# Reordered start of a four-layer graph-attention kernel: first nodes and layer 0's weights ahead, the other layers' preparation behind the first projections

## The chip, the cores and the metric

One core of one Trainium2 chip runs the whole kernel. The metric is device microseconds (us) of one execution. Of the kernel before, three first runs gave a median of 3268.11 us (3267.7 to 3269.8). Runs are sorted into a fast and a slow state by their time. Each comparison of times is made within one call, on one chip; a comparison of two profiles can be across calls and chips, and two profiles of one kernel differ by about 1 us at the start (see b0_before and c0_after).

## The reference, cut to what matters

```python
# x (16, 1024, 256) f32, adj (16, 1024, 1024) int32 in {0, 1}
def layernorm(x): m, v = mean(x), var(x); return (x - m) / sqrt(v + 1e-5)

# layers 0, 1, 2 (they differ in the edge function and in an elu at the end)
h   = maximum(layernorm(x), 0)
Wh  = h @ W                                  # (1024, 256) @ (256, 256) for each of 16 batches
e   = leaky_relu((Wh @ a1)[:, :, None] + (Wh @ a2)[:, None, :], 0.2)
att = softmax(where(adj == 0, NEG, e), axis=-1)
x   = x + einsum('bij,bjo->bio', att, Wh)
# layer 3: four heads of 64, a_src and a_dst of shape (4, 5, 64) of which only type 0 is met,
# then relu, bias, a layernorm with gamma and beta over each head, and x + that
```

## The kernel before

The kernel handles 16 batches as two interleaved streams. A batch needs its nodes `x_b` (1 MB), its adjacency as eight tiles of 128 rows (loaded with a cast to bf16, squared for a check on ACT, transposed on PE, cast into `mask` on ACT), then for each layer a projection (`project`), edge weights (`weigh`, on DVE) and the sums over neighbours (`attend`, on PE). The instruction order on each engine is not the order of the source: a scheduler settles it when the kernel is built.

```python
    ident_b = const.tile([P, P], BF, name="ident_b")
    nc.vector.tensor_copy(ident_b, ident)               # needed by every adjacency transpose
    ...
    def load(b: int):
        xs[b] = nodes.tile([P, NI, D], F32, name="x_b")
        nc.sync.dma_start(xs[b], x[b].rearrange("(i p) f -> p i f", p=P))
        masks[b] = nodes.tile([P, NI, N], U8, name="mask")
        def fetch(i: int):
            fetched[i] = adjs.tile([P, N], BF, name="adj_i")       # three buffers
            nc.gpsimd.dma_start(fetched[i], adj[b, ts(i, P), :])
        for i in range(AHEAD):                                     # AHEAD = 2
            fetch(i)
        yield
        for i in range(NI):                                        # NI = 8
            if i + AHEAD < NI:
                fetch(i + AHEAD)
            adj_i = fetched.pop(i)
            nc.scalar.activation(every, adj_i, AF.Square, ..., accum_out=squares[:, b, i : i + 1])
            turned = psum.tile([P, NI, P], BF, name="misc", bufs=3)
            for j in range(NI):
                nc.tensor.transpose(turned[:, j, :], adj_i[:, ts(j, P)], ident_b)
            nc.scalar.copy(masks[b][:, :, ts(i, P)], turned)
            yield

    # loads of W0..W3, bias, gamma, beta on SP: all ahead of the first nodes
    for l in range(3): nc.sync.dma_start(W[l][:, :, :D], ...)
    ...
    for _ in load(0):                                              # x_b of batch 0 and its masks
        pass
    nc.vector.tensor_scalar_add(beta, beta, -2.0)
    with tc.tile_pool(name="prep", bufs=2) as prep:                # all layers: W x a on DVE
        for l in range(3): ...  # load a_b; tensor_tensor_reduce(prod, W, a_b, accum_out=wa)
        for s, name in enumerate(("L3_a_src", "L3_a_dst")): ...    # load 640 KB, use a fifth of it
        ...                     # columns of W from wa, and a check of the norms on PE
    ...
    def batch(b: int):
        ...
        for n in range(NI // 2 + 2):                               # project layer 0, four pairs of tiles
            for pair in range(max(n - 2, 0), min(n + 1, NI // 2)):
                yield from islice(pairs[pair], 1)
        ...
        V = yield from attend(0, V, finish0, 1)
```

In `attend` each edge weight tile `w[:, j, :]` (128x512, made on DVE) feeds four sums of 128 rows:

```python
            for j in range(NI):
                nc.tensor.matmul(acc, w[:, j, ts(i % NG, P)], V[:, j, : D + 1],   # 128x257, f32
                                 start=(j == 0), stop=(j == NI - 1))
```

## Time and profile before

The timeline gives the marks that the argument runs on. All are us from the start of the span.

| mark | before |
|---|---|
| first statistics of the nodes (nodes landed) | 17.77 |
| adjacency tile 0 turned | 16.3 |
| tile 3 fetched / tile 7 fetched | 16.9 / 27.3 |
| first projection of layer 0 | 38.62 |
| first edge weight | 46.89 |
| product records 1, 17 and 41 of the first sums | 48.46, 53.14, 58.36 |
| end | 3266.97 |

A "record" is one matmul entry of the trace, in the group of the sums `acc<-V,weights`. The program has 3072 such products (3 layers, 16 batches, 64 each) and the profile lists 6144, so a product of 128x257 in f32 is two records. One weight tile thus feeds eight records in the end. This line of the timeline of the kernel before (columns: start, us, engine, line, operation, output and inputs, shapes, count) is a reading that the prediction passed over:

```profile
50.47 9.79 PE L346 MATMUL acc<-V,weights 128*128 128x257 f32 x44
```

From 50.47 us on PE takes 44 records without a gap, 0.22 us each. The weights are not all there yet at that time, but PE is full.

### The profile page before, as it was taken

The page shows a single profiled execution, that of the slowest core. Times are in us where ns is not written, and L with a number is a line of the kernel's source. Part 1 is how long each engine was busy: PE and PEld are TensorE (multiplying, and loading weights), DVE is VectorE, ACT ScalarE, POOL GpSimd, SP SyncE. Part 2 cuts the span into 40 slices and gives each one's busy share as a digit, 9 for nine tenths or more (in the row PEclk, how much of TensorE's full clock was granted, in tenths as well). Part 3 has the DMA queues.
Part 4 walks back from the last instruction along what each step waited for, and adds up shares of the span by engine and source line. Part 5 has one row for each costly group of instructions (what it writes and reads, how often), then busy time and mean ns, then how long its engine had stood idle before and what let it go on. Part 6 is the DMA issues. An engine that isn't in the chain of part 4 may idle for free.

```text
span 3267.0 us, 38466 instructions
## 1 busy us (share of the span) xinstructions
PE 3075.9 (94%) x13702; PEld 2129.5 (65%) x13702; DVE 2546.5 (78%) x6140; ACT 969.5 (30%) x2081; POOL 1086.2 (33%) x1286
## 2 busy tenths in 40 slices
PE   6999999999999999999999999999999999999987
PEld 5776766657666676666766667676676766767562
DVE  5778787777877778877788877888778787787767
ACT  3423323232332323323233232322323223232121
POOL 1323424233242332423334233342323423233242
PEclk8999999999999999999999999999999999999998
DMA  4101101011010111100111010110101101000000
GB/s 118 27 4 17 33 12 41 7 16 30 14 39 7 17 29 17 36 10 13 30 17 36 10 17 28 15 36 13 39 4 17 33 13 40 4 14 13 1 13 14
DMA packets 55190, 73.18 MB, mean 22 GB/s; under 512 B 4048, under 2 KB 37968, under 8 KB 54992
## 3 DMA queue, kind: packets, MB, share of 16 engines
q0 software_dynamic: 18432, 33.56, 7.0%
q1 hardware_dynamic: 36560, 37.10, 3.6%
q8 instruction: 110, 1.80, 0.2%
q14 instruction: 88, 0.72, 0.1%
HBM read 87.43 MB, written 16.78 MB: 32 GB/s over the span
## 4 chain that ended last, share of the span: by engine, by line
PE 70%; DVE 18%; POOL 6%; issue 2%; ACT 2%; DMA 1%; SPq 0%; ACTq 0%; POOLq 0%
PE acc L346 31%; PE acc L427 22%; PE projected L242 11%; DVE weights L262 8%; PE misc L235 2%; PE misc L254 2%; POOL x_b L282 2%; DVE centered L227 2%; DVE stats L222 2%; POOL rstd L213 1%; PE misc L122 1%; DVE above L280 1%; DVE above L281 1%; DMA adj_i<-in_adj_dram 1%; POOL y L407 1%
## 5 line engine op out<-in xcount | busy, mean ns | idle before, releaser
L346 PE MATMUL acc<-V,weights 128*128 128x257 f32 x6144 | 1440.8, 384 | 8.4 <-DVE weights L262 7.0
L346 PEld LDWEIGHTS acc<-V,weights 128*128 128x128 f32 x6144 | 1139.5, 191 | 205.0 <-DVE weights L262 38.6
L427 PE MATMUL acc<-weights,V 128*65 128x512 f32 x2048 | 913.2, 594 | 0.3 <-DVE weights L262 0.3
L262 DVE SCALAR_TENSOR_TENSOR weights<-row,ex,mask 128x512 f32<-128x512 f32 x1024 | 744.9, 776 | 36.7 <-ACT row L258 36.7
L262 DVE SCALAR_TENSOR_TENSOR weights<-row,V,mask 128x512 f32<-128x512 f32 x768 | 593.4, 815 | 49.3 <-ACT row L258 47.9
L213 POOL TENSOR_TENSOR rstd<-rstd,minus_half 128x2 f32<-128x2 f32 (+1 forms) x320 | 330.2, 1034 | 883.3 <-DVE rstd L212 834.9
L427 PEld LDWEIGHTS acc<-weights,V 128*65 128x65 f32 x2048 | 279.4, 138 | 499.4 <-issue 477.2
L242 PE MATMUL projected<-W,hT 128*128 128x259 f32 (+1 forms) x2048 | 522.3, 397 | 40.8 <-DVE V L297 24.9
L242 PEld LDWEIGHTS projected<-W,hT 128*128 128x128 f32 x2048 | 388.1, 195 | 137.0 <-DVE V L297 37.5
L282 POOL TENSOR_TENSOR x_b<-x_b,above 128x256 f32<-128x256 f32 x256 | 222.1, 868 | 478.9 <-DVE above L281 436.6
L278 ACT ACTIVATE below<-acc,inv 128x256 f32<-128x256 f32 x256 | 121.0, 473 | 657.1 <-DVE inv L271 463.5
L222 DVE BATCH_NORM_STATS2 stats<-x_b 128x6 f32<-128x256 f32 x512 | 209.3, 415 | 126.0 <-POOL x_b L282 121.1
L235 PE MATMUL misc<-ident,centered 128*128 128x128 f32 x1024 | 168.5, 281 | 75.7 <-DVE centered L227 70.3
L237 ACT COPY hT<-misc 128x512 f32<-128x512 f32 x256 | 147.2, 588 | 299.6 <-PE misc L235 298.9
L227 DVE TENSOR_SCALAR centered<-x_b,mv 128x256 f32<-128x256 f32 x512 | 229.6, 451 | 4.7
L431 ACT COPY sums<-acc 65x512 f32<-65x512 f32 x128 | 74.1, 579 | 513.9 <-PE acc L427 512.4
L235 PEld LDWEIGHTS misc<-ident,centered 128*128 128x128 f32 x1024 | 120.8, 143 | 128.2 <-DVE centered L227 107.9
L258 ACT COPY row<-misc 128x512 f32<-128x512 f32 x224 | 129.8, 587 | 196.2 <-PE misc L254 196.0
L106 POOL DMA_DIRECT2D adj_i<-in_adj_dram x128 | 77.6, 606 | 287.4 <-ACT sums L431 214.6
L280 DVE TENSOR_SCALAR above<-acc,inv 128x256 f32<-128x256 f32 x256 | 122.8, 480 | 61.8 <-ACT below L278 60.9
L392 POOL TENSOR_TENSOR y<-y,bias 128x512 f32<-128x512 f32 x64 | 90.5, 1414 | 234.2 <-DVE y L439 215.9
L293 ACT ACTIVATE V<-projected,rstd 128x3 f32<-128x3 f32 x384 | 99.3, 263 | 228.0 <-PE projected L242 227.4
(70 smaller groups left out, 2311.4 us busy)
## 6 DMA issues: line engine op xcount, KB each, us to landing
adj_i<-in_adj_dram POOLq DMA_DIRECT2D x128, 256.0 KB, 3.9
x_b<-in_x_dram SPq DMA_DIRECT2D x16, 1024.0 KB, 7.9
out_dram<-y SPq DMA_DIRECT2D x32, 512.0 KB, 3.6
W<-in_L_gnn_W_dram SPq DMA_DIRECT2D x3, 256.0 KB, 3.6
a_b<-in_L_gnn_a_dram SPq DMA_DIRECT2D x3, 256.0 KB, 7.4
a_b<-in_L_gnn_a_src_dram SPq DMA_DIRECT2D x1, 640.0 KB, 8.4
a_b<-in_L_gnn_a_dst_dram SPq DMA_DIRECT2D x1, 640.0 KB, 10.2
W<-in_L_gnn_W_dram SPq DMA_DIRECT2D x2, 128.0 KB, 9.4
```

The lines of the kernel that those rows point to most:

```text
L213: nc.gpsimd.tensor_tensor(r, r, minus_half.to_broadcast([P, n]), op=ALU.pow)
L222: nc.vector.bn_stats(stats, xb[:, 2 * pair + n, :])
L227: nc.vector.tensor_scalar(centered[:, n, :], xb[:, 2 * pair + n, :], mv[:, n, 0:1], 0.0, op0=ALU.subtract, op1=ALU.max,)
L235: nc.tensor.transpose(turned[:, k, ts(n, P)], centered[:, n, ts(k, P)], ident)
L237: nc.scalar.copy(hT, turned)
L242: nc.tensor.matmul(projected, hT[:, k, ts(n, P)], W[l][:, k, :], start=(k == 0), stop=(k == NK - 1),)
L258: nc.scalar.copy(r, turned)
L262: nc.vector.scalar_tensor_tensor(w[:, j, :], r, c(j), mask[:, j, ts(half, HALF)], op0=op, op1=ALU.mult)
L280: nc.vector.tensor_scalar(above, acc[:, :D], inv, 0.0, op0=ALU.mult, op1=ALU.max)
L282: nc.gpsimd.tensor_add(xi, xi, above)
L346: nc.tensor.matmul(acc, w[:, j, ts(i % NG, P)], V[:, j, : D + 1], start=(j == 0), stop=(j == NI - 1),)
L427: nc.tensor.matmul(accT, V3[:, j, h, :], w[:, j, :], start=(j == 0), stop=(j == NI - 1))
```

## The change

Its intent is to start the real work of the first batch earlier: the nodes of batch 0 and layer 0's W and a go to the head of the load queue, in the source the other layers' loads and DVE preparation come behind the first projections, and so does batch 0's mask work. Layer 3's two vectors are loaded without the four fifths that nobody reads, and temporary tiles come from pools that exist anyway. The diff, cut to its core:

```diff
@@ the loads and the preparation become a generator
-    for l in range(3):
-        nc.sync.dma_start(W[l][:, :, :D], ins[f"L{l}_W"].rearrange("(k p) o -> p k o", p=P))
-    ... (W3, bias, gamma, beta)
-    for _ in load(0):
-        pass
-    nc.vector.tensor_scalar_add(beta, beta, -2.0)
-    with tc.tile_pool(name="prep", bufs=2) as prep:
-        ... (products of W and a of all layers)
-            nc.sync.dma_start(
-                a_b3.rearrange("p h t e -> p (h t e)"), on_all_partitions(ins[name], H * T * E)
-            )
+    def prepare():
+        scratch = edges.tile([P, NI, HALF], F32, name="weights")
+        def fetch(l: int): ...                       # W and a of layer l
+                    bass.AP(tensor=first.tensor, offset=first.offset, ap=[[0, P], [T * E, H], [1, E]]),
+        fetch(0)
+        for l in range(3):
+            if l == 0:
+                yield
+            fetch(l + 1)
+            ... (products of W and a of layer l)
+            extend(l)
+            yield
+        ... (layer 3, and only then beta, and the check of the norms)
@@ def batch(b)
+        if b == 0:
+            next(preparing)                          # layer 0's preparation only
@@ after the projections of layer 0
+        if b == 0:
+            for _ in chain(loading, preparing):      # masks of batch 0, then layers 1 to 3
+                pass
@@ before the streams start
+    loading, preparing = load(0), prepare()
+    next(loading)                                    # x_b of batch 0, tiles 0 and 1
+    next(preparing)                                  # W0, a0
```

More of the change, by code (lines that the diff above doesn't have):

```diff
@@ L23 @@
 from contextlib import ExitStack
-from itertools import islice
+from itertools import chain, islice
 import concourse.bass as bass
@@ L99, in load @@
         nc.sync.dma_start(xs[b], x[b].rearrange("(i p) f -> p i f", p=P))
-        masks[b] = nodes.tile([P, NI, N], U8, name="mask")
+        mask = masks[b] = nodes.tile([P, NI, N], U8, name="mask")
         fetched = {}
@@ L122, in load @@
                 nc.tensor.transpose(turned[:, j, :], adj_i[:, ts(j, P)], ident_b)
-            nc.scalar.copy(masks[b][:, :, ts(i, P)], turned)
+            nc.scalar.copy(mask[:, :, ts(i, P)], turned)
             yield
-    W = [const.tile([P, NK, D + e], F32, name=f"W{l}") for l, e in enumerate(EXT)]
-    for l in range(3):
-        nc.sync.dma_start(W[l][:, :, :D], ins[f"L{l}_W"].rearrange("(k p) o -> p k o", p=P))
-    for k in range(NK):
-        nc.sync.dma_start(
-            W[3][:, k, :D].rearrange("p (h e) -> p h e", h=H),
-            ins["L3_W"][:, ts(k, P), :].rearrange("h p e -> p h e"),
-        )
+    edges = ctx.enter_context(tc.tile_pool(name="edges", bufs=4))
+    rows = ctx.enter_context(tc.tile_pool(name="rows", bufs=4))
+    single = ctx.enter_context(tc.tile_pool(name="single", bufs=1))
+    work = ctx.enter_context(tc.tile_pool(name="work", bufs=3))
+    small = ctx.enter_context(tc.tile_pool(name="small", bufs=6))
+    W = [const.tile([P, NK, D + e], F32, name=f"W{l}") for l, e in enumerate(EXT)]
+    wa = const.tile([P, NK, 3 + H, 2], F32, name="wa")
     bias = const.tile([P, D], F32, name="bias")
@@ L137, in short_path @@
     beta = const.tile([P, D], F32, name="beta")
-    for t, a in ((bias, ins["L3_bias"]), (gamma, ins["L3_gamma"]), (beta, ins["L3_beta"])):
-        nc.sync.dma_start(t, on_all_partitions(a, D))
-    for _ in load(0):
-        pass
-    nc.vector.tensor_scalar_add(beta, beta, -2.0)
-    wa = const.tile([P, NK, 3 + H, 2], F32, name="wa")
-    with tc.tile_pool(name="prep", bufs=2) as prep:
-        for l in range(3):
-            a_b = prep.tile([P, 2, D], F32, name="a_b")
-            nc.sync.dma_start(
-                a_b.rearrange("p s o -> p (s o)"), on_all_partitions(ins[f"L{l}_a"], 2 * D)
-            )
-            for k in range(NK):
-                for s in range(2):
-                    prod = prep.tile([P, D], F32, name="prod")
-                    nc.vector.tensor_tensor_reduce(
-                        prod, W[l][:, k, :D], a_b[:, s, :], op0=ALU.mult, op1=ALU.add,
-                        scale=1.0, scalar=0.0, accum_out=wa[:, k, l, s : s + 1],
-                    )
-        for s, name in enumerate(("L3_a_src", "L3_a_dst")):
-            a_b3 = prep.tile([P, H, T, E], F32, name="a_b3")
-            nc.sync.dma_start(
-                a_b3.rearrange("p h t e -> p (h t e)"), on_all_partitions(ins[name], H * T * E)
-            )
-            for k in range(NK):
-                prod3 = prep.tile([P, H, E], F32, name="prod3")
-                nc.vector.tensor_mul(
-                    prod3, W[3][:, k, :D].rearrange("p (h e) -> p h e", h=H), a_b3[:, :, 0, :]
-                )
-                nc.vector.tensor_reduce(wa[:, k, 3:, s], prod3, AX.X, ALU.add)
+    def prepare():
         forms = [
@@ L177, in short_path, with extend @@
         ]
-        for l, form in enumerate(forms):
+        scratch = edges.tile([P, NI, HALF], F32, name="weights")
+        def extend(l: int):
             n = EXT[l] // 3
-            for c, factor in enumerate(form):
+            for c, factor in enumerate(forms[l]):
                 nc.vector.tensor_scalar_mul(
@@ L185, in short_path, with fetch @@
                 )
-        wa2 = prep.tile([P, NK, 3 + H, 2], F32, name="wa2")
-        nc.vector.tensor_mul(wa2, wa, wa)
+        def fetch(l: int):
+            if l < 3:
+                nc.sync.dma_start(
+                    W[l][:, :, :D], ins[f"L{l}_W"].rearrange("(k p) o -> p k o", p=P)
+                )
+                nc.sync.dma_start(scratch[:, l, :], on_all_partitions(ins[f"L{l}_a"], 2 * D))
+                return
+            for k in range(NK):
+                nc.sync.dma_start(
+                    W[3][:, k, :D].rearrange("p (h e) -> p h e", h=H),
+                    ins["L3_W"][:, ts(k, P), :].rearrange("h p e -> p h e"),
+                )
+            for s, name in enumerate(("L3_a_src", "L3_a_dst")):
+                first = ins[name]
+                nc.sync.dma_start(
+                    scratch[:, 3, ts(s, D)].rearrange("p (h e) -> p h e", h=H),
+                    bass.AP(tensor=first.tensor, offset=first.offset, ap=[[0, P], [T * E, H], [1, E]]),
+                )
+            for t, a in ((bias, ins["L3_bias"]), (gamma, ins["L3_gamma"]), (beta, ins["L3_beta"])):
+                nc.sync.dma_start(t, on_all_partitions(a, D))
@@ new lines, in prepare @@
+        fetch(0)
[3 more added lines that the diff above has]
+            fetch(l + 1)
+            for k in range(NK):
+                for s in range(2):
+                    prod = work.tile([P, D], F32, name="above", bufs=2)
+                    nc.vector.tensor_tensor_reduce(
+                        prod, W[l][:, k, :D], scratch[:, l, ts(s, D)], op0=ALU.mult, op1=ALU.add,
+                        scale=1.0, scalar=0.0, accum_out=wa[:, k, l, s : s + 1],
+                    )
+            extend(l)
+            yield
@@ new lines, in prepare @@
+        for s in range(2):
+            for k in range(NK):
+                prod = work.tile([P, D], F32, name="above", bufs=2)
+                nc.vector.tensor_mul(prod, W[3][:, k, :D], scratch[:, 3, ts(s, D)])
+                nc.vector.tensor_reduce(
+                    wa[:, k, 3:, s], prod.rearrange("p (h e) -> p h e", h=H), AX.X, ALU.add
+                )
+        extend(3)
+        nc.vector.tensor_scalar_add(beta, beta, -2.0)
+        groups = (3 + H) * 2
+        wa2 = small.tile([P, NK, groups], F32, name="wa2", bufs=1)
@@ L189, in short_path @@
+        nc.vector.tensor_mul(wa2, wa.rearrange("p k g s -> p k (g s)"), wa.rearrange("p k g s -> p k (g s)"))
         norms = psum.tile([P, 3 + H, 2], F32, name="misc", bufs=3)
@@ L191, in short_path @@
             nc.tensor.matmul(
-                norms.rearrange("p g s -> p (g s)"), ones,
-                wa2[:, k].rearrange("p g s -> p (g s)"), start=(k == 0), stop=(k == NK - 1),
+                norms.rearrange("p g s -> p (g s)"), ones, wa2[:, k],
+                start=(k == 0), stop=(k == NK - 1),
             )
-        both = prep.tile([P, 3 + H], F32, name="both")
+        both = small.tile([P, 3 + H], F32, name="both", bufs=1)
         nc.vector.tensor_reduce(both, norms, AX.X, ALU.add)
-        worst = prep.tile([P, 1], F32, name="worst")
+        worst = small.tile([P, 1], F32, name="worst", bufs=1)
         nc.vector.tensor_reduce(worst, both, AX.X, ALU.max)
         nc.vector.tensor_scalar(bad, worst, REACH * REACH / (2.0 * D), None, op0=ALU.is_gt)
-    edges = ctx.enter_context(tc.tile_pool(name="edges", bufs=4))
-    rows = ctx.enter_context(tc.tile_pool(name="rows", bufs=4))
-    single = ctx.enter_context(tc.tile_pool(name="single", bufs=1))
-    work = ctx.enter_context(tc.tile_pool(name="work", bufs=3))
-    small = ctx.enter_context(tc.tile_pool(name="small", bufs=6))
+        yield
     def inverse_root(var: bass.AP, n: int, eps: float, scale: float = 1.0) -> bass.AP:
```

## The prediction

> **What bounds the kernel now.** I read the page's engine totals first, then busy time by stretch, then the waits and the timeline of the first 60 us, because the change touches nothing later.
>
> ```profile
> PE 3075.9 (94%) x13702; PEld 2129.5 (65%) x13702; DVE 2546.5 (78%) x6140; ACT 969.5 (30%) x2081; POOL 1086.2 (33%) x1286
> ```
>
> PE is busy 94% of 3267 us, so 191 us are idle in the whole program. The stretches (columns: us, then busy us of PE, PEld, DVE, ACT, POOL, granted clock, DMA share, GB/s) say where:
>
> ```profile
> 0.00:16.00 16.00, 0.67 (x7) 0.77 (x8) 0.68 (x5) 2.52 (x3) 2.52 (x9) 1.00 0.88 220
> 16.00:24.00 8.00, 2.47 (x25) 2.21 (x23) 6.23 (x34) 5.48 (x8) 1.62 (x3) 0.84 0.94 277
> 24.00:36.00 12.00, 5.52 (x42) 4.35 (x40) 5.71 (x33) 10.16 (x15) 3.82 (x6) 0.50 1.06 271
> 36.00:50.50 14.50, 14.00 (x61) 11.34 (x62) 8.13 (x22) 8.05 (x20) 1.99 (x3) 0.80 0.26 43
> ```
>
> Before 36 us PE works 0.67 + 2.47 + 5.52 = 8.7 us: 27 us of idleness, all that a better start can win from. In the same 36 us the 16 DMA engines are about 0.9 busy or more, ACT is nearly full from 24 on, and DVE is busy 12.6 us. The waits of PE before 50.5 us:
>
> ```profile
> PE misc L122 <- DVE ident_b L84: 15.3, 1, 15.3
> PE misc L122 <- DMA adj_i<-in_adj_dram: 10.5, 4, 5.5
> ```
>
> The timeline shows the chain behind them:
>
> ```profile
> 14.85 0.29 DVE L143 TENSOR_SCALAR beta<-beta 128x256 f32<-128x256 f32 x1 [13.65 <-DMA beta<-in_L_gnn_ln_beta_dram]
> 15.06 0.22 DVE L84 CAST ident_b<-ident 128x128 bf16<-128x128 f32 x1
> 15.33 2.72 PE L122 MATMUL misc<-ident_b,adj_i 128*128 128x128 bf16 x24 [15.33 <-DVE ident_b L84]
> ...
> 16.88 0.54 POOL L106 DMA_DIRECT2D adj_i<-in_adj_dram  x1 [13.25 <-PE misc L122]
> ...
> 33.88 1.03 PE L122 MATMUL misc<-ident_b,adj_i 128*128 128x128 bf16 x8 [1.02 <-DMA adj_i<-in_adj_dram]
> ...
> 36.04 2.79 PE L235 MATMUL misc<-ident,centered 128*128 128x128 f32 x12 [0.36 <-DVE mv L223]
> ...
> 46.89 1.41 DVE L262 SCALAR_TENSOR_TENSOR weights<-row,V,mask 128x512 f32<-128x512 f32 x2
> ```
>
> DVE waits 13.65 us for beta, needed only in layer 3; the cast ident_b stands behind it, the transposes of adjacency tile 0 behind that, and the fetch of tile 3 (three buffers) behind those. Tile 7 is turned at 33.88; only then does the first projection start, and the edge weights of layer 0 start at 46.89. The eighth weight tile is ready at about 53.9 (four by 50.8, four more from 51.14), the first sum of eight products ends then, and PE is nearly full from there on. So **53.9 us is the mark to move**.
>
> **What the Trainium skill says.** (1) "DMA: Bandwidth & Descriptors", Queues, rings and completion order: each DMA engine takes turns between its queues, packet by packet. The trace agrees: from 4 to 10 us the software queue (adjacency) has about 0.7 of the engine time and the SP queue 0.3, though SP has plenty queued. (2) Same page, Specifications: under 512 B a DMA does not reach line rate. The trace's packets agree mildly: 256 B take 19 ns, 1 KB 52 ns, so 13 against 20 B/ns. (3) "TensorE: Matmul & The Clock Gate", Part 1: an idle PE runs at half clock and needs a busy window of 3.4 us to get the full one. The trace agrees: clock 0.50 in 24 to 36 us, 1.00 from 41.9 us, with short stretches of half clock, 3.4 or 6.8 us each, later.
>
> **The change part by part.** The order of instructions of both kernels, taken from the builds, differs only at the start: the first 204 rows of PE, 122 of DVE, 35 of ACT, 23 of POOL; after that each engine's list is the same. So whatever is won is a rigid shift of the rest.
>
> *Transfers.* Packet times of the trace: 1 KB 52 ns, 2 KB 90, 5 KB 200, 256 B 19, an adjacency packet 172. Layer 3's two vectors shrink from 256 packets of 5 KB (256 x 200 / 16 engines = 3.2 us) to 1024 of 256 B (1.2 us): 2.0 us saved. The rest is the same data in another order. Nodes go first: 1024 packets, 500 of them before the first adjacency data (seen at 3.8 us here), the others in turn with 384 adjacency packets at 224 ns a pair over 16 engines, 5.4 us, so nodes land at about 9.7 us instead of 17.77. Layer 0's W (0.8) and a (0.7) follow: 11.3 us. Each later layer takes 1.5 us; W3 1.2, a3 1.2, bias, gamma, beta 1.2: done at about 18, with the next two batches' nodes until 25.
>
> *DVE from 9.7 us*, in the new order: two tiles' statistics and centering to 11.8; layer 0's four products at 0.35 and three small writes to 13.7; ident_b; three pairs' statistics at 1.35 to 18.3; layer 1's preparation and then two evictions (L297, 0.54 each) to 21.1; then layers 2 and 3 with the other six evictions mixed in: 1.9 + 3.2 (eight of 0.37 to 0.42) + 3.2 and small writes, to about 30.
>
> *PE and the mask.* Here the gain is given back in part. In PE's new list tile 0's transposes stand behind pair 1's projections, which wait for the eviction of pair 0 (two projected buffers) at 21.1. So tile 0 is turned by 22.6 rather than 16.9, and tile 3 is fetched 6 us *later* than before. Tile 1's last two transposes stand behind pair 3's projections: 27.6. Tiles 4, 5 and 6 are then fetched at 27.7, 28.8 and 29.8 and land about 4 us later (3.9 median on the page, since the DMA engines are then free; it was 6.6 under load).
>
> *ACT* is then the last limit. It is in order: it waits for tile 3 and then has the last small evictions, until 29. From there three mask casts at 1.0 (to 32.0), then tiles 4 to 7 at 1.15 + 0.19 for the square and 1.0 for the cast, 2.15 a tile by their starts in the timeline: 8.6 us, to 40.7 (tile 7, fetched once tile 4's square is done at 33.4, has landed by 37.5, so it fits). The row copy (0.6) after it: 41.3 to 42.
>
> *Result.* First weight from 42.0 at the latest, eight at 0.67 now with no evictions between: 47.4. Mark moved by 53.9 - 47.4 = 6.5 us. Against it, PE was hardly busy from 30 to 42 us and starts the sums at half clock; while the weights pace it (0.67 against some 0.43 for a product at half clock) nothing is lost, afterwards up to one window's rest; I take 0.7 us. **Sum: 6 us won, 3268.1 - 6 = 3262 us, 0.2%.** The lists' sums of work hardly change (2.0 us of DMA work, off the path from there on).
>
> **Rivals.** (a) *The adjacency chain is not delayed*, because evictions come earlier than I have them: then tile 7 lands near 32 and weights start near 36, as if the last ACT part began 5 us sooner; the win is 11 to 12 us, 3257. For it: DMA work before tile 7 is down and PE sat idle. Against it: the order of PE's list, and 20 us of DVE work between 9.7 and 30. (b) *The chain is worse*: each of tiles 4 to 7 has its full landing time in series, two to a round, and x_b of the next batches lies in the same engines, so that landing stays at 6.6 us. Tile 7 then lands at 42 to 43 and weights start at 46: nothing won, 3268. For it: fetches wait on PE and ACT for their buffer. Against it: by my queue sum the SP queue is empty at 25. (c) *The shift is swallowed later*: a wait on something with a time of its own. Against it: lists are the same, and nothing later depends on the clock of the start, save the half-clock stretches, whose number (17 in this trace, most of 3.4 us and so costing at most 1.7 us) can change by one or two: plus or minus 2 us. (d) *A gain above 2%* needs 65 us, twice what PE idles before 36 us: excluded; *a loss of 2%* has no mechanism.
>
> **Range and chances.** Centre 3262 between rivals (a) at 3257 and (b) at 3268; with the window effect and the runs' own spread (3267.7 to 3269.8) I take 3256.5 to 3267 for 8 in 10. Faster by over 2%: 0.005; within 2%: 0.99; slower: 0.005.
>
> **What would show it right or wrong.** In the changed profile: nodes land near 10 us and the first statistics start then (wrong if after 13); the first projection near 16 instead of 38.6; tile 3's fetch near 22.6 and tile 7's near 33 (if tile 3's is before 19, rival a); ACT full from 29 to 41 with casts and squares; the first edge weight near 42 (36 is rival a, 46 rival b); the half clock lasting until after 42; the granted clock and waits past 60 us as now. The prediction fails as a whole if the first weight comes at the time I say and the end does not move by the same amount within 2 us.

## The result, and the profile after

| | median | range | runs |
|---|---|---|---|
| before | 3269.14 us | 3267.7 to 3274.43 | 6 |
| after | 3266.11 us | 3263.96 to 3269.45 | 6 |

The ratio is 0.9989 (95% interval 0.9976 to 1.0002). Here and below, a ratio is the mean time of one kernel's fast runs over the mean of the other's of the same rounds, so it is not quite the ratio of the medians quoted.

The page's engine totals of the kernel after, and its stretches (us, then busy us of PE, PEld, DVE, ACT, POOL, granted clock, DMA share, GB/s):

```profile
PE 3075.4 (94%) x13702; PEld 2130.8 (65%) x13702; DVE 2546.2 (78%) x6140; ACT 969.4 (30%) x2081; POOL 1085.1 (33%) x1286
```

```profile
0.00:16.00 16.00, 3.64 (x12) 2.58 (x13) 7.17 (x40) 4.14 (x6) 4.86 (x12) 1.00 0.90 239
16.00:24.00 8.00, 8.00 (x48) 6.59 (x47) 7.75 (x36) 5.20 (x13) 1.45 (x3) 1.00 0.98 236
24.00:36.00 12.00, 5.24 (x50) 4.18 (x46) 3.08 (x12) 7.66 (x13) 2.11 (x4) 0.78 0.80 154
36.00:42.50 6.50, 3.78 (x20) 3.27 (x20) 1.25 (x5) 5.89 (x10) 1.58 (x3) 0.50 0.87 129
42.50:50.50 8.00, 7.96 (x25) 6.55 (x26) 7.27 (x11) 3.56 (x7) 0.00 (x0) 0.67 0.10 19
```

The totals are the same work. Before 24 us PE now does 11.64 us instead of 3.14, and from 16 to 24 us it is full. Then PE is half idle, 9.0 busy of 18.5 us from 24 to 42.5, while the masks are made; and the last row shows what will matter most: PE is full from 42.5 us, at a granted clock of 0.67.

The waits of PE before 50.5 us (us in total, times, longest):

```profile
PE misc L250 <- DVE rstd L227: 8.3, 1, 8.3
PE misc L122 <- DMA adj_i<-in_adj_dram: 6.7, 3, 3.2
PE misc L250 <- DVE centered L242: 4.0, 1, 4.0
```

The 15.3 us wait on `ident_b` is gone; PE's first wait is now 8.3 us for the nodes' statistics, and the waits for adjacency data fell from 10.5 to 6.7 us.

The timeline after, at the places that answer the one of before:

```profile
6.72 0.75 DVE L237 BATCH_NORM_STATS2 stats<-x_b 128x6 f32<-128x256 f32 x2 [5.52 <-DMA x_b<-in_x_dram]
10.88 0.43 DVE L189 CUSTOM_DVE_ANT_0 above<-W,weights 128x256 f32<-128x256 f32 x1 [2.36 <-DMA weights<-in_L_gnn_a_dram]
...
20.44 0.50 PE L122 MATMUL misc<-ident_b,adj_i 128*128 128x128 bf16 x6
21.43 0.57 POOL L106 DMA_DIRECT2D adj_i<-in_adj_dram  x1 [4.02 <-ACT V L310]
...
28.34 1.15 ACT L117 ACTIVATE wide<-adj_i,minus_half 128x1024 bf16<-128x1024 bf16 x1 [5.29 <-DMA adj_i<-in_adj_dram]
...
29.77 2.84 ACT L123 CAST mask<-misc 128x1024 uint8<-128x1024 bf16 x3
34.04 0.53 POOL L106 DMA_DIRECT2D adj_i<-in_adj_dram  x1 [3.64 <-ACT wide L117]
37.89 1.03 PE L122 MATMUL misc<-ident_b,adj_i 128*128 128x128 bf16 x8 [3.25 <-DMA adj_i<-in_adj_dram]
...
41.73 8.04 DVE L277 SCALAR_TENSOR_TENSOR weights<-row,V,mask 128x512 f32<-128x512 f32 x12 [1.45 <-ACT row L273]
42.54 12.82 PE L363 MATMUL acc<-V,weights 128*128 128x257 f32 x46 [0.61 <-DVE weights L277]
```

The nodes are there 11 us earlier and layer 0's products start 8 us earlier (10.88 against 18.83), the first projections begin at 14.62 us, but the masks are now the last to come: tile 0 is turned at 20.9, the fetch of tile 3 waits for that, and tile 3 lands 6.9 us later, with the next batches' nodes (issued at 16.32) in the same queues. ACT sits idle for 5.29 us until its square of tile 3 can start at 28.34; the last evictions of the projections and three casts stand behind that square in ACT's order, so the casts begin at 29.77, and tile 7 lands at 37.9. The first weight comes at 41.73, 5.16 us earlier than before. The last line is to be held against its counterpart of before: 46 records in 12.82 us are 0.28 us each, against 44 in 9.79, 0.22 each.

Counted from the 41st record on, where both kernels run at full clock, the kernel after is 4.47 us ahead; at record 101 4.50, at record 501 (229 us) 4.34, at the end of these two profiled executions 3.73. So a start won by 6.75 us (end of the eighth weight, 53.87 to 47.12) gave 4.5 us.

### The profile page after: what moved, and what is told of

The parts are those of the page before. It is cut to its first block, busy times and chain, and to the rows that moved or that the text cites. A ratio compares the mean times of both kernels' runs of the same rounds, so it can differ in the third digit from the quotient of the medians.

```text
span 3263.2 us, 38469 instructions
## 1 busy us (share of the span) xinstructions
PE 3075.4 (94%) x13702; PEld 2130.8 (65%) x13702; DVE 2546.2 (78%) x6140; ACT 969.4 (30%) x2081; POOL 1085.1 (33%) x1286
## 4 chain that ended last, share of the span: by engine, by line
PE 71%; DVE 17%; POOL 6%; issue 3%; ACT 2%; DMA 1%; POOLq 0%; ACTq 0%; SPq 0%; DVEq 0%
PE acc L363 32%; PE acc L447 22%; PE projected L257 11%; DVE weights L277 7%; PE misc L250 2%; PE misc L269 2%; POOL x_b L297 2%; DVE centered L242 2%; DVE stats L237 2%; POOL rstd L228 1%; PE misc L122 1%; DVE above L295 1%; DVE above L296 1%; POOL y L427 1%; ACT below L293 1%
```

## The experiments

Every profile is judged by the same mark: the shift of record 41 (58.36 us in the first profile of before, minus the same record's start). It is one profile against one profile, so differences of about 1 us in it are not told from chance. All edits of one part stand below as short diffs; "after" is the changed kernel.

### The changed kernel once more (c0_after)

No edit. 

> The changed kernel again, for a tighter ratio and as the yardstick of the other runs of this call. Its first profile put the first edge weight of layer 0 at 41.7 us (46.9 before) and the 40th product of the first sums 4.5 us earlier than before, and this shift of 4.5 us was still there at 285 us. Theory A (rigid shift plus noise of the half-clock stretches): the mean of five rounds is 3 to 5.5 us faster than before. Theory B (the start's win is partly given back in the steady state): 1 to 2.5 us faster, with the shift at 285 us again near 4.5. The noise of a single run, some 2 us, may leave this open.

Measured: 3265.96 us (3263.87 to 3267.15, 5 runs) against 3270.00 of before (9 runs), ratio 0.9983 (0.9969 to 0.9996). First weight 42.51 (0.8 later than in the first profile), full clock back at 49.51 instead of 47.81 us, and so the shift of record 41 only 3.23. The interval leaves out 1, in the first result it did not; the medians differ by 3.0 and 4.0 us, the ratios stand for 3.6 and 5.6. The gain is small, some 3 to 6 us, and its size at the start already varies with the clock.

### PE kept busy ahead of the first sums (e2_warm)

```diff
+            if b == 0 and i == 6:
+                spare = psum.tile([P, 2 * P], BF, name="projected")
+                for _ in range(24):
+                    nc.tensor.transpose(spare[:, :P], adj_i[:, :P], ident_b)
```

> The changed kernel with 24 extra bf16 transposes of adjacency tile 6 (into a spare PSUM tile that nobody reads), so that PE is busy while it waits for tile 7, from about 34.6 to 37.9 us. Theory (half clock costs 2.2 us of the win): first edge weight unchanged at 41.7 (41.4 to 42.3), but the full clock is granted by 44.5 instead of 47.8, and the shift of the 40th product against the kernel before grows from 4.5 to 6.0 to 7.2 us. Rival (the weights' pace sets the first sums, not the clock): the full clock comes early and the shift stays at 4.5 to 5. Time: 1.5 to 2.5 us under the changed kernel by the theory, within 1 by the rival.

Measured: in its timeline the spare transposes fill the wait for tile 7, and the sums run at full rate from their first record:

```profile
34.85 2.72 PE L127 MATMUL projected<-ident_b,adj_i 128*128 128x128 bf16 x24
38.17 0.62 PE L122 MATMUL misc<-ident_b,adj_i 128*128 128x128 bf16 x8 [0.60 <-ACT wide L117]
...
42.41 9.88 PE L367 MATMUL acc<-V,weights 128*128 128x257 f32 x44 [1.87 <-DVE weights L281]
```

Full clock from 37.39 us; 16 records in 3.62 us where the changed kernel took 6.16. The first weight stayed where it was (41.61), but the shift of record 41 rose from 4.47 to 7.10 us. So half clock cost the change 2.6 us (the first 16 records alone give 2.5). The time, 3266.25 us (ratio 0.9987, 0.9973 to 1.0000), does not show it: see the noise below.

### Three casts moved from ACT to DVE (e5_dve_casts)

```diff
-            nc.scalar.copy(mask[:, :, ts(i, P)], turned)
+            if b == 0 and 0 < i < 4:
+                nc.vector.tensor_copy(mask[:, :, ts(i, P)], turned)
+            else:
+                nc.scalar.copy(mask[:, :, ts(i, P)], turned)
```

> The changed kernel with the mask casts of tiles 1, 2 and 3 on DVE instead of ACT. In the changed kernel ACT does these three from 29.8 to 32.6 us, ahead of tile 4's square, whose end lets tile 7 be fetched (34.04). Theory (ACT's order sets tile 7's fetch and with it the first weight): fetch of tile 7 at 32.5 to 33.3, landing 36.3 to 37.2, first weight 40.2 to 41.0, about 1 us earlier than 41.7. Rival (tile 7's landing and the first weight are set by the DMA engines or by PE): first weight stays at 41.4 to 42. Time: 1 us less by the theory, too little for the timing; the profile decides.

Measured: tile 7 fetched at 33.55 instead of 34.04, first weight 41.20 instead of 41.73, shift 4.90; 3264.10 us (3261.20 to 3267.53), ratio 0.9983 (0.9968 to 0.9999). Taking three casts of 1 us from ACT gained half a us in the marks, less than two profiles of one kernel differ. The theory's times were missed (tile 7 fetched at 32.5 to 33.3, first weight 40.2 to 41.0). The chain's timeline of this run shows why:

```profile
30.74 3.47 DVE L124 CAST mask<-misc 128x1024 uint8<-128x1024 bf16 x3
32.01 3.12 PE L122 MATMUL misc<-ident_b,adj_i 128*128 128x128 bf16 x24 [3.02 <-DVE mask L124]
33.55 0.53 POOL L106 DMA_DIRECT2D adj_i<-in_adj_dram  x1 [3.09 <-PE misc L122]
37.35 1.04 PE L122 MATMUL misc<-ident_b,adj_i 128*128 128x128 bf16 x8 [2.22 <-DMA adj_i<-in_adj_dram]
```

The casts on DVE began only at 30.74, 1 us later than on ACT, and took 3.47 us instead of 2.84. They stood behind two evictions (DVE from 29.83, after 4.55 us of waiting for ACT), and ACT's part of these stood behind its square of tile 3, which waited for the landing until 28.40, as in the changed kernel. Tile 4's square came 2.2 us earlier on ACT (30.27 against 32.48), so ACT no longer set the last fetch; but PE's transposes need the PSUM tiles that the casts free, whichever engine does them, and the fetch now waited for the transposes of tile 4. So the run does not clear ACT in the changed kernel. It shows a second path, through the PSUM tiles, that ended here only half a us before ACT's did there, and that the casts of both runs began behind the landing of tile 3.

### Masks interleaved with the projections (e6_interleaved)

```diff
         for n in range(NI // 2 + 2):
             for pair in range(max(n - 2, 0), min(n + 1, NI // 2)):
                 yield from islice(pairs[pair], 1)
+            if b == 0:
+                next(loading, None)
```

> The changed kernel with the adjacency tiles of batch 0 emitted between the steps of the first projections instead of behind all of them; nothing else. Theory (part of the win is given back because tile 0's transposes stand behind pair 1's projections in PE's order, so that tile 3 is fetched at 21.4 us instead of 16.9): tile 0 is turned at 13 to 14, tile 3 fetched at 13.5 to 15, tile 7 lands at 29 to 33, first weight at 34.5 to 38 us, a shift of the 40th product of 7 to 11 us against before, and a time 3 to 6 us under the changed kernel. Rival (the DMA engines, with the next batches' nodes among the adjacency tiles, limit it anyway): tile 7 lands at 35 or later and the first weight comes at 39 to 42, the time within 2 us of the changed kernel.

Measured: tile 3 fetched at 14.3 instead of 21.4, first weight 38.93, shift of record 41 8.36 us; 3265.27 us (3260.82 to 3267.25), ratio 0.9979 (0.9966 to 0.9993). The shift is in the theory's range; the first weight lies between theory and rival; the time, 0.7 us under the changed kernel by the medians, does not show the 3 to 6 us that were expected. The earlier fetches did not all pay:

```profile
16.16 1.18 SPq L99 DMA_DIRECT2D x_b<-in_x_dram  x2
17.04 0.57 POOL L106 DMA_DIRECT2D adj_i<-in_adj_dram  x1
...
27.25 0.62 PE L122 MATMUL misc<-ident_b,adj_i 128*128 128x128 bf16 x8 [3.36 <-DMA adj_i<-in_adj_dram]
```

Tile 4, fetched at 17.04 us, was turned only at 27.25, having landed just then: 10 us, with 2 MB of nodes of batches 1 and 2 issued just ahead of it.

### The kernel before against itself (b0_before)

No edit. 

> The kernel before against itself, for a second profile of it. In six profiles so far the time from the 41st edge weight (at 126 to 134 us) to the end was 3130 to 3139 us and went with the time at half clock in between (55 to 79 us), though all engines have the same instructions there; the phase of the grid of 3.41 us on which the clock changes differed from run to run. Theory (this is noise of the grid's phase, the same for every kernel): the ratio is within 0.1% of 1, first weight at 46.5 to 47.5 us as before, and the stretch from the 41st weight to the end between 3130 and 3139 us, not by need the 3132.7 of the first profile. Rival (the changed kernels have a slower steady state of their own): this profile again 3131.5 to 3133.5.

Measured: 3271.41 us against 3273.08, ratio 1.0003 (0.9989 to 1.0016). Its first weight came at 45.94 us, 0.95 earlier than in the first profile, and its end 2.05 us later. So the start alone varies by 1 us from run to run, and the rest by more. The first weight missed the theory's 46.5 to 47.5. The rival fell: from the 41st edge weight (133.25 us) to the end it took 3135.8 us, outside 3131.5 to 3133.5.

Why the rest varies: in all 14 profiles the time from record 41 to the end lies between 3206.1 and 3215.7 us, though the kernels differ in hardly more than the start. It goes with the time spent at half clock between these points (68 to 99 us): correlation 0.89, 0.25 us per us of half clock. The half-clock stretches are multiples of 3.41 us, on a grid whose phase differed from profile to profile. This is a correlation, not an experiment; I found no way to set the phase.

### Beta's add moved in the source (e1_beta_late)

```diff
-    nc.vector.tensor_scalar_add(beta, beta, -2.0)
     wa = const.tile(...)
     ...
+    nc.vector.tensor_scalar_add(beta, beta, -2.0)     # behind the preparation
```

> The kernel before with one line moved: beta - 2 is computed behind the preparation instead of ahead of everything on DVE. No transfer changes place. Theory (the wait for beta holds back ident_b and with it the fetch of tile 3): ident_b at about 3 us, tile 0 turned at 9.5 to 10, tile 3 fetched at 9.5 to 11 instead of 16.9, tile 7 turned at 30 to 32.5 instead of 34.9 since the DMA engines are near full all the time, and the first weight 2 to 4.5 us earlier than 46.9; time 2 to 4 us less than before. Rival (the wait was beside the point, as the DMA engines limit the start): tile 7 turned within 1 us of 34.9, the first weight within 1 us of 46.9, time the same within 1 us.

Measured: every mark of the start within 0.13 us of the kernel before; 3269.76 us, ratio 0.9995 (0.9982 to 1.0009). Nothing was tested: the scheduler put the add ahead of `ident_b` on DVE again, where it had been (14.74 us in this run, `ident_b` at 14.95). The run is a second repeat of before, and a lesson; e1c below is the experiment that was meant.

### The next batches' nodes held back (e7_nodes_behind)

```diff
 # e6_interleaved, and in load(b), ahead of the load of x_b:
+        if b in (1, 2):
+            nc.gpsimd.tensor_copy(xs[b][:, 0, :1], squares[:, 0, 4:5])   # waits for tile 4's square
```

> The interleaved kernel, and the nodes of batches 1 and 2 now wait for the square of tile 4 (a copy of one column into their tiles, which the transfer then overwrites). In the interleaved kernel tile 4 took 10 us from fetch to landing while these 2 MB were moved. Theory (they crowd out the adjacency tiles): tiles 3 to 6 land within 3.5 to 6 us of their fetch, tile 4 by 23, tile 7 is turned by 27 to 31 instead of 35.1, the first weight comes at 32.5 to 36 instead of 38.9, limited by ACT's own sum of work, and the shift of the 40th product against before is 10.5 to 14 us. Rival (ACT's and POOL's order limit it, not the DMA engines): first weight at 37.5 to 39.5. Time 2 to 5 us under the interleaved kernel by the theory, which the noise of some 2 us a run may hide.

Measured: tile fetches at 14.6, 17.3, 20.0, 22.7 and 25.3, first weight 36.78, shift 9.95 us; 3263.82 us (3260.13 to 3265.80), ratio 0.9972 (0.9958 to 0.9985). First weight and shift fell just short of the theory (36 us at the latest, 10.5 at the least), and tile 7 was turned at 32.9, not by 31: the nodes, issued at 25.00, now met its fetch:

```profile
25.00 1.05 SPq L101 DMA_DIRECT2D x_b<-in_x_dram  x2
25.27 0.54 POOL L108 DMA_DIRECT2D adj_i<-in_adj_dram  x1 [0.18 <-DMA adj_i<-in_adj_dram]
...
32.94 1.03 PE L124 MATMUL misc<-ident_b,adj_i 128*128 128x128 bf16 x8 [4.75 <-DMA adj_i<-in_adj_dram]
36.78 5.39 DVE L279 SCALAR_TENSOR_TENSOR weights<-row,V,mask 128x512 f32<-128x512 f32 x8 [1.44 <-ACT row L275]
```

### Held-back nodes and spare transposes together (e8_both)

```diff
 # e7_nodes_behind with the 24 spare transposes of e2_warm
```

> The same with the 24 spare transposes on PE behind tile 6. Theory: the first weight as in the kernel without them, within 0.7 us, and the full clock granted at the first sums, so that the 40th product comes 1 to 2.5 us earlier than without them: a shift against before of 12 to 16 us, the best version of the study, 0.3 to 0.5% faster than before. Rival (the clock is already full at the first sums once the projections lie among the adjacency tiles, as they partly do in the interleaved kernel): no difference beyond 0.5 us.

Measured: first weight 38.77, 2 us later than e7, shift 7.58; 3265.20 us, ratio 0.9983 (0.9969 to 0.9997). A miss: the scheduler put the spare transposes behind tile 7's, on the path:

```profile
32.36 1.04 PE L124 MATMUL misc<-ident_b,adj_i 128*128 128x128 bf16 x8 [4.20 <-DMA adj_i<-in_adj_dram]
33.19 2.77 PE L129 MATMUL projected<-ident_b,adj_i 128*128 128x128 bf16 x24
37.00 1.97 PE L275 MATMUL misc<-ident,V 128*128 128x128 f32 x8 [0.26 <-DVE both L222]
```

### The nodes behind tile 6's square (e9_nodes_later)

```diff
-            nc.gpsimd.tensor_copy(xs[b][:, 0, :1], squares[:, 0, 4:5])
+            nc.gpsimd.tensor_copy(xs[b][:, 0, :1], squares[:, 0, 6:7])
```

> Edit: as e7_nodes_behind, but the 2 MB of nodes of batches 1 and 2 wait on tile 6's square instead of tile 4's, so that tile 7's fetch too is issued ahead of them. Theory (in e7 tile 7 took 7.7 us, 25.3 to 32.9, because the nodes were queued with it; alone a tile takes some 3.8 to 4.2 us): tile 7 fetched at 25.3 +- 0.5 and landed by 30.0; first weight at 33.0 to 34.5 (e7 36.78), the shift of the 40th product against the kernel before 12 to 14 us where the clock is full at the first sums, 10.5 to 12 where it is half; time .996 to .9975 of the kernel before. Rival 1 (the preparation on DVE takes its place as the bound): tile 7 early, but first weight at 35.5 or later, and the wait before the row's transposes names DVE. Rival 2 (the nodes of batch 1, then fetched some 3 us later, hold back the second stream): a gain in the marks that is gone again by the 500th product.

Measured: 3260.07 us (3257.22 to 3260.71) against 3272.18, ratio 0.9962 (0.9949 to 0.9976). The marks of the start came as the theory had them. The shift came out larger: the clock was half at the first sums (16 records in 5.34 us), for which it gave 10.5 to 12 us, and 13.87 is what it gave for full clock.

```profile
25.37 0.53 POOL L108 DMA_DIRECT2D adj_i<-in_adj_dram  x1 [2.22 <-PE misc L124]
29.79 0.62 PE L124 MATMUL misc<-ident_b,adj_i 128*128 128x128 bf16 x8 [1.98 <-DMA adj_i<-in_adj_dram]
29.97 1.41 SPq L101 DMA_DIRECT2D x_b<-in_x_dram  x2
...
33.15 8.04 DVE L279 SCALAR_TENSOR_TENSOR weights<-row,V,mask 128x512 f32<-128x512 f32 x12 [1.75 <-ACT row L275]
```

Tile 7 is fetched at the same time as in e7 and lands after 4.4 us instead of 7.7, and the first weight comes 3.63 us earlier, at 33.15. The only edit was the moment at which the nodes were issued, so what had lengthened the landing was the shared transfer. This rests on one profile of each, but the difference is three times what repeats differ by. Shift of record 41: 13.87 us, 14.55 at record 501. The second stream did not suffer (rival 2), nor did DVE become the bound (rival 1).

### The same with tile 6's transposes done three times (e10_later_warm)

```diff
-            for j in range(NI):
+            for j in list(range(NI)) * (3 if b == 0 and i == 6 else 1):
```

> Edit: as e9, with tile 6's eight transposes done three times over into the same PSUM tile (16 spare ones, 0.08 us each at full and 0.13 at half clock), so that PE has less idle time before the rows. Theory (half clock at the first sums costs some 2 us and comes from PE's idle time ahead of them): full clock within 3 us of the first weight, and the shift of the 40th product 1 to 2.5 us above that of e9. Rival (spare transposes lie at the head of the row chain and delay tile 7's, and one idle window decides the clock anyway): first weight 0.5 to 1.5 us later than in e9, and the shift of the 40th product the same as e9's or less.

Measured: 3257.93 us (3256.87 to 3261.62), ratio 0.9961 (0.9947 to 0.9975). First weight 33.20, full clock from 37.30 (e9: 37.57), the first 16 records in 5.17 us (e9: 5.34), shift 13.98. The theory fell and the second half of the rival held: 16 spare transposes (some 0.9 us more than the eight alone) kept the full clock until 33.88 us instead of 30.75, but the window in which the first sums begin (to 37.3) was at half clock all the same; and they cost nothing. The two are equal; e9 is the simpler one.

### The wait on beta alone taken from the kernel before (e1c_beta_last)

```diff
-    nc.vector.tensor_scalar_add(beta, beta, -2.0)
 # at the end of the preparation, where `worst` is its last result:
+        two = prep.tile([P, 1], F32, name="two")
+        nc.vector.tensor_scalar(two, worst, 0.0, -2.0, op0=ALU.mult, op1=ALU.add)
+        nc.vector.tensor_scalar(beta, beta, two, None, op0=ALU.add)
```

> Edit: the kernel before with one thing altered: beta's add takes its -2 from a tile written at the end of the preparation, so that it can't stand ahead of ident_b on DVE; the order on PE, ACT and POOL is unchanged, and no load moves. It asks how much of the gain is the removal of that one wait. Theory (the wait on beta holds the whole mask chain): tile 0 turned at 9.5 instead of 16.3, tile 3 fetched at 11 to 12 instead of 16.9; tile 7's transposes at 29.5 to 31 instead of 33.88, first weight 42.0 to 44.0 instead of 46.89: a shift of the 40th product of 2.5 to 4.5 us, that is over half of the gain of 4.5. Rival (the fetches that come earlier share the DMA queues with the nodes and L3's 5 KB packets, and give it back): tile 3 fetched 5 us earlier but landed at most 2.5 us earlier, first weight after 45.0, shift of the 40th product under 2 us. Time .9985 to .9995 by the theory, .9995 to 1.0005 by the rival; the noise of the steady state may hide either.

Measured: 3269.09 us (3268.57 to 3272.25), ratio 0.9994 (0.9980 to 1.0007); shift of record 41 2.02 us, short of the theory's 2.5 and at the edge of the rival's, whose reason was wrong too: tile 3 landed 5.2 us earlier (18.39 against 23.58). Its timeline:

```profile
2.61 0.23 DVE L84 CAST ident_b<-ident 128x128 bf16<-128x128 f32 x1 [1.42 <-POOL ident masks.py:199]
10.77 0.54 POOL L106 DMA_DIRECT2D adj_i<-in_adj_dram  x1 [7.14 <-ACT wide L117]
18.39 1.04 PE L122 MATMUL misc<-ident_b,adj_i 128*128 128x128 bf16 x8 [6.32 <-DMA adj_i<-in_adj_dram]
29.22 0.43 DVE L153 CUSTOM_DVE_ANT_0 prod<-W,a_b 128x256 f32<-128x256 f32 x1 [1.81 <-DMA a_b<-in_L_gnn_a_dram]
29.44 1.03 PE L122 MATMUL misc<-ident_b,adj_i 128*128 128x128 bf16 x8 [1.46 <-DMA adj_i<-in_adj_dram]
34.36 2.42 PEld L235 LDWEIGHTS misc<-ident,centered 128*128 128x128 f32 x12 [1.51 <-POOL rstd L213]
```

`ident_b` is there 12.5 us earlier and tile 3 is fetched 6.1 us earlier; of this tile 7's transposes keep 4.4 us (29.44 against 33.88). Then 2.7 of the 4.4 are lost to a wait that had been hidden: the last products of the preparation wait for a load until 29.22 (27.35 before; that the earlier tile fetches delay it in the shared queues is an inference), and the statistics stand behind them, so PE's first transposes of the nodes come at 34.4 rather than 36.04, only 1.7 us earlier. Taking away the wait on beta without moving the preparation is worth 2.0 us at record 41, about half of what the change gains there (4.47 and 3.23 in its two profiles); with 1 us between repeats, it can't be said closer.

### The masks ahead of the projections in the changed kernel (e3_mask_first)

```diff
         if b == 0:
             next(preparing)
+            for _ in loading:
+                pass
```

> Edit: the changed kernel with its loads and its late preparation, but all of the mask work of batch 0 put ahead of the first projections again (as the kernel before had it). It asks whether the projections ahead of the masks are worth anything by themselves. On ACT the copies of the projections' input now stand behind all eight casts, as before. Theory (the mask chain is the only thing that sets the first weight once nodes and layer 0 are there): tile 0 turned at 10.7 to 12, tile 7 landed at 28 to 31, then four pairs of projections (some 8 us on PE and ACT) still have to follow it: first weight 38 to 41, at or a little ahead of the changed kernel's 41.7. Rival (the projections behind the masks cost more than the masks ahead gain): first weight 42 to 45. Clock: PE is busy with projections just ahead of the first sums, so full clock by the first sums, and the shift of the 40th product 5.5 us or more by the theory, 2 to 5 by the rival.

Measured: 3270.35 us (3267.29 to 3271.41), ratio 0.9993 (0.9979 to 1.0006); first weight 43.54, shift of record 41 3.35 us. The rival held. Tile 0 was turned only at 14.2 (`ident_b` came at 12.87 on DVE, behind layer 0's products) and tile 4, fetched at 17.43 with the nodes of the next batches in the queue, was turned from 27.02. Its first weight came 1.0 to 1.8 us later than in the two profiles of the changed kernel (42.51 and 41.73), but its sums had full clock from 36.24 on, and at record 41 it lies between them (3.23 and 4.47). So the projections ahead of the masks bring the first weight forward a little, and half clock takes most of that back; a net gain is not shown. In one order the crowded fetch of tile 4 ends the start, in the other the late turn of tile 0.

### All of them together

The times are noisy by some us, the shift of record 41 by about one. If the shift is carried rigidly to the end, 3270 us times one minus the ratio should give it back:

| kernel | shift of record 41, us | 3270 x (1 - ratio), us |
|---|---|---|
| e1_beta_late | 0.13 | 1.6 |
| b0_before | 0.94 | -1.0 |
| e1c_beta_last | 2.02 | 2.0 |
| c0_after | 3.23 | 5.6 |
| e3_mask_first | 3.35 | 2.3 |
| after (first result) | 4.47 | 3.6 |
| e5_dve_casts | 4.90 | 5.6 |
| e2_warm | 7.10 | 4.3 |
| e8_both | 7.58 | 5.6 |
| e6_interleaved | 8.36 | 6.9 |
| e7_nodes_behind | 9.95 | 9.2 |
| e9_nodes_later | 13.87 | 12.4 |
| e10_later_warm | 13.98 | 12.8 |

Every row agrees within 3 us, over shifts of 0 to 14 us; the interval of each ratio is some 4 us to either side. So the start is carried to the end, and nothing later swallows it as far as this can tell; single profiles and medians of five runs can't resolve 2 us. The best kernel, e9 or e10, is faster than before by 0.4%, two to three and a half times the change's own gain (0.11 and 0.17% in its two measurements).

## Why the prediction was right, and where it was not

The predicted 3262.0 us was measured as 3266.11, inside the range of 3256.5 to 3267.0 and in the class with 0.99. That alone proves little: the range is 10.5 us wide, 3266.11 lies 0.9 us from its upper end, and against the 3269.14 us of before the gain was 3.0 us where 6 were forecast. So the steps count:

- *The same work, and a rigid shift.* Shown: the totals of the engines agree to 1.3 us, and in the table above the shift arrives at the end within 3 us in all 13 measurements.
- *Transfers.* The nodes landed at 6.7 us, not 9.7: the adjacency data came later than assumed (first packets at 5.9 us, not 3.8), so the nodes had the queues nearly alone. Layer 0's vectors at 10.88 (11.3 predicted) and the first projection at 14.62 (16) are near.
- *The order on PE delays the masks, and gives part of the gain back.* Shown: tile 0 turned at 20.9 (22.6), tile 3 fetched at 21.4 (22.6), later than before by 4.5 us. e6, which undoes just this, lies 3.9 us further ahead at record 41.
- *ACT is the last limit.* The times were hit: casts from 29.77 (29), tile 7 fetched at 34.04 (33.4) and landed at 37.9 (37.5), first weight 41.73 (42.0 at the latest). ACT did wait for tile 3 and did the last evictions next, as predicted, and its squares and casts set tile 7's fetch. But taking three casts off ACT won only half a us (e5): a path through the PSUM tiles then set the fetch, and the prediction did not have it. As the casts came later on DVE and took longer, the run does not say how far behind ACT that path lies in the changed kernel.
- *Rivals (a) and (b).* Neither came in the changed kernel. But (a)'s condition, a chain that is not delayed, was built in e6 to e10, and its first weight near 36 was reached (36.78 in e7) and passed (33.15 in e9). The crowding that (b) feared was real too, but it met other tiles: in the changed kernel tile 7 landed in 3.8 us and tile 3 in 6.9, in e6 and e7 a tile took 10 and 7.7.
- *The half-clock term, 0.7 us, was the step that failed.* The text said that while the weights pace PE nothing is lost, "0.67 against some 0.43 for a product at half clock". The 0.43 us is one record, and a product is two, so 0.87 us at half clock; and with two sums side by side a weight tile feeds about three records (24 records for eight weights), 1.3 us at half clock against 0.67 us for the weight. At full clock the two are even, 0.65 to 0.67. So at half clock PE, not DVE, paced the first sums, and half clock cost it in full: 16 records in 6.16 us against 3.62 in e2. (Of the changed kernel's 16, four took the last 0.89 us at full clock and twelve the 5.27 us of half clock before, 0.44 each.) Measured loss 2.6 us.
- *The mark itself* was a little off for the same reason. In the kernel before PE is full from 50.47 us with four records done, which is worth a gapless start at 50.47 - 4 x 0.217 = 49.60 us; after, it starts at 42.54. That is 7.06 us, and e2, at full clock, measured 7.10. The prediction's 53.9 - 47.4 = 6.5 was near by luck. So 6.5 - 0.7 = 5.8 should have read 7.1 - 2.6 = 4.5.
- *"The prediction fails as a whole if the end does not move by the same amount within 2 us".* In the two profiles the first weight moved by 5.16 and the end by 3.73, within 2 us. The mark of the eighth weight moved by 6.75, so by that reading it was 3 us: the half-clock term again.

What stays open: I found no way to set the phase of the clock grid, so its share of the run noise is a correlation only. The change has several parts, and only the wait on beta (e1c) and the order of masks and projections (e3, e6) were taken apart; what the earlier nodes, the late preparation and the smaller loads of layer 3 (2.0 us of transfer time by the prediction's sum) are worth each was not measured.

## What to carry to other kernels

At the start of a kernel, ask what each early transfer will share its engines with: holding back 2 MB that nobody needs yet was worth at least as much here (e6 to e9, 5.5 us) as the reordering that was meant to help (4.5 and 3.2). Removing one wait at the head of a chain gains only up to the next one that it hid (4.4 us became 1.7 in e1c); and before an experiment is run on an order in the source, the built order has to be read, because the scheduler need not follow the source. When a shift is too small for the clock noise, measure it at a fixed instruction soon after the change, not at the end, and take a second profile to see how far that mark moves by itself (about 1 us here).

## What the Trainium skill lacked or had wrong

- "TensorE: Matmul & The Clock Gate", Part 1, says that the ramp penalty is under 1% of a typical span and that one should not fit a specific cold count. True of the span here (2.6 of 3266 us), but it took 2.6 of the 7.1 us that the change won, and the time at half clock goes with a run noise of several us: for a change of a few us it is a term of its own.
- The same page says that the idle state is the throttled one. The durations agree, but the clock view of a profile does not show it. The page warns that the clock's trace events can be unreliable, but not that the time ahead of the first one is missing: the first record in the kernel after lies at 17.09 us, everything ahead of that reads 1.00, though eight projection records from 14.62 on took 3.14 us and eight from 18.63 on 1.97.
- "DMA: Bandwidth & Descriptors", Latency and other measured facts, gives about 1 us to the first byte of a software-issued DMA. With 1 MB of nodes queued ahead on the other queue, the first packets of the fetch issued at 1.42 us came between 5.5 and 6 us (between 3.5 and 4 in the kernel before).
- No page says how many records of a trace an f32 product of 128x257 leaves: here it is two, of 0.217 us each at full and some 0.43 us at half clock; reading one record as a product was this prediction's error.
